# A selective scan laid out by (state, channel) pairs: spread and summed by zero-one matrices on TensorE, product with C on GpSimd, halves of 512 tokens

## The chip, the core and the metric

The kernel runs on one core of a Trainium2 chip. A core has five engines with a queue each, and each queue is worked off in order: TensorE (PE; matrix products, its weight loads are shown apart as PEld), VectorE (DVE), ScalarE (ACT), GpSimd (POOL) and SyncE (SP, here only DMA issues). Engines wait for each other through semaphores. Tensors lie in SBUF, or in PSUM, where matmuls write: eight banks of 512 fp32 columns for each of 128 partitions. GpSimd reads and writes SBUF only.

The metric is the device time of one execution in microseconds (us), median of several runs. A profile of one execution gives the span from the first to the last instruction.

## The reference

Two layers on x of 4 x 256 tokens with 512 features. The first is attention and a gated FFN, the same in both kernels. The second, where the change lies, is a selective state recurrence beside a mixture of LoRA experts:

```python
proj = hidden_states @ in_proj_w            # 512 -> 2*1024
x, z = jnp.split(proj, 2, axis=-1)
xc = silu(conv_b + sum_k conv_w[k] * shifted(x, k))      # 4 taps along time
ssm_p = einsum('bdl,ed->ble', xc, x_proj_w)              # 32 + 16 + 16
dt_r, Bm, Cm = rmsnorm of the three parts
dt = softplus(einsum('blr,dr->bdl', dt_r, dt_proj_w) + dt_bias)
A = -jnp.exp(A_log)                                      # (1024, 16)
def step(h, inp):                                        # along time
    x_t, dt_t, B_t, C_t = inp
    dA = jnp.exp(dt_t[..., None] * A)
    h = dA * h + dt_t[..., None] * B_t[:, None, :] * x_t[..., None]
    y = jnp.einsum('bdn,bn->bd', h, C_t)
    return (h, y)
y = (ys + D_param * xc) * silu(z);  out = y @ out_proj_w
```

There are 1024 channels, 16 states for each, 4 sequences of 256 tokens: 1024 x 16 x 1024 values of h, one after the other along time within each sequence.

## The kernel before

Tiles are declared and the instructions written in program order; a scheduler orders each engine's queue by priorities and its own estimates, so the order in the queues differs from the text. A tile pool has a number of buffers per tag; a new tile waits until its buffer's last reader is done.

Up to L373 layer 0 runs (attention L196 to L280, FFN L282 to L321). At L348 to L371 the weights of layer 1 are loaded and `aneg` (minus exp of A_log) is made, then `down(1)` ends the FFN.

Layer 1 works by sequence (`b`, 256 tokens), channels on partitions in eight chunks (`c`) of 128, taken in pairs:

- `normed` (L391): layer norm and transposes to `xn`.
- `conv_pair` (L396): for two chunks, in-projection on TensorE (L404), a copy and the last tap on ScalarE, three taps on VectorE (L412), silu.
- `ssm_params` (L418): dt_r, B and C; the B and C rows go to DRAM and come back by DMA, copied to all 128 partitions as `rows` (L435 to L442; 8 loads of 512 KB a sequence).
- `gates` (L447): silu(z) for two chunks. `steps` (L458): softplus as a chain over ScalarE and GpSimd (L481 to L486), giving `dt` and `du` = dt * xc.
- `scan_chunk` (L491): a channel per partition. For four groups of four states (`NG`), a tile of 4 x 256 columns: `da` = exp(dt * A) on ScalarE (L501, one activation a state, the first column of each state is kept 0 so that the scan starts anew), `bx` = B * du (L504), the scan `h` (L508), `bx` = h * C (L512), all three on VectorE, and the sum over states as four matmuls with the identity into `y` (L514). At the end y times the gate (L516).
- `experts` (L518), `finish` (L584; out-projection, sum and store).

The loop (L602 to L624) sets the work of the next sequence (convolution, parameters, first steps) between the chunks of this one. PSUM: three banks `mm`, three `s`, two `y`. Three decay buffers, three `bx`, two `h`.

Of the kernel before, what the change touches and what calls it, by code (L numbers as in the profile page):

```python
# [17 lines left out]
P = 128  # L18
# [10 lines left out]
NG = 4  # L29
# [11 lines left out]
def block_kernel(  # L41
# [307 lines left out]
    inx = w1.tile([P, DC, HC, P], F32, name="inx")  # L349
# [17 lines left out]
    ow = w1.tile([P, DC, D], F32, name="ow")  # L367
    nc.sync.dma_start(ow, ow_d)
    aneg = w1.tile([P, DC, NST], F32, name="aneg")
    nc.scalar.activation(aneg, vec[:, :, V_AL : V_AL + NST], AF.Exp)  # L370
# [8 lines left out]
    psmm = ctx.enter_context(tc.tile_pool(name="psmm1", bufs=3, space=PSUM))  # L379
    pss = ctx.enter_context(tc.tile_pool(name="pss", bufs=3, space=PSUM))  # L380
    psy = ctx.enter_context(tc.tile_pool(name="psy", bufs=2, space=PSUM))
    scr = ctx.enter_context(tc.tile_pool(name="scr", bufs=2, space=DRAM))
# [3 lines left out]
    for i in range(3):  # L386
        t = act.tile([P, NG, S], F32, name=f"decay{i}")
        nc.gpsimd.memset(t[:, :, 0:1], 0.0)
        decay.append(t)

    def normed(b):  # L391
        xn = act.tile([P, HC, S], F32, tag="xn1T", name="xn1T", bufs=2)
        layernorm_T((2 * b, 2 * b + 1), act, psmm, xn, 1)
        return xn

    def conv_pair(xn, xc, c0):  # L396

        px = psmm.tile([P, 2, S], F32, tag="mm", name="px")
        pad = act.tile([P, 2, KC - 1 + S], F32, tag="pad", name="pad")
        acc = act.tile([P, 2, S], F32, tag="acc", name="acc")  # L400
        nc.gpsimd.memset(pad[:, :, 0 : KC - 1], 0.0)
        for i in range(2):
            for hc in range(HC):
                mm(px[:, i, :], lhsT=inx[:, c0 + i, hc, :], rhs=xn[:, hc, :],  # L404
                   start=(hc == 0), stop=(hc == HC - 1))
        nc.scalar.copy(pad[:, :, KC - 1 :], px)
        for i in range(2):
            v = vec[:, c0 + i, :]
            nc.scalar.activation(acc[:, i, :], px[:, i, :], AF.Identity, bias=v[:, V_CB : V_CB + 1],  # L409
                                 scale=v[:, V_CW + KC - 1 : V_CW + KC])  # L410
            for k in range(KC - 1):
                nc.vector.scalar_tensor_tensor(  # L412
                    acc[:, i, :], pad[:, i, k : k + S], v[:, V_CW + k : V_CW + k + 1],
                    acc[:, i, :], ALU.mult, ALU.add,
                )
        nc.scalar.activation(xc[:, c0 : c0 + 2, :], acc, AF.Silu)

    def ssm_params(xc):  # L418

        pp = pss.tile([P, S], F32, tag="s", name="pp")  # L420
        for c in range(DC):
            mm(pp[:64, :], lhsT=xpw[:, c, :], rhs=xc[:, c, :], start=(c == 0), stop=(c == DC - 1))  # L422
        sp = act.tile([64, S], F32, tag="sp", name="sp")
        nc.vector.tensor_copy(sp, pp[:64, :])
        sq = act.tile([64, S], F32, tag="sq", name="sq")
        nc.scalar.activation(sq, sp, AF.Square)
        pq = pss.tile([P, S], F32, tag="s", name="pq1")
        mm(pq[:64, :], lhsT=cst[:64, C_BLK : C_BLK + 64], rhs=sq, start=True, stop=True)
        rs = act.tile([64, S], F32, tag="sq", name="rs1")
        nc.scalar.activation(rs, pq[:64, :], AF.Sqrt, bias=eps[:64, 1:2])  # L430
        nc.vector.reciprocal(rs, rs)  # L431
        nrm = act.tile([64, S], F32, tag="nrm", name="nrm", bufs=2)
        nc.vector.scalar_tensor_tensor(nrm, sp, lnw[:, 0:1], rs, ALU.mult, ALU.mult)
        bc = scr.tile([2 * NST, S], F32, tag="bc", name="bc")
        nc.sync.dma_start(bc, nrm[RK:, :])  # L435
        rows = []
        for g in range(NST // NG):
            pair = []
            for k in range(2):
                t = act.tile([P, NG, S], F32, tag=f"bc{g}{k}", name=f"bc{g}{k}")  # L440
                r0 = k * NST + g * NG
                nc.sync.dma_start(t, bc[r0 : r0 + NG, :].partition_broadcast(P))  # L442
                pair.append(t)
            rows.append(pair)
        return nrm, rows

    def gates(xn, c0):  # L447

        sz = act.tile([P, 2, S], F32, tag="sz", name="sz", bufs=2)
        pz = psmm.tile([P, 2, S], F32, tag="mm", name="pz1")  # L450
        for i in range(2):
            for hc in range(HC):
                mm(pz[:, i, :], lhsT=inz[:, c0 + i, hc, :], rhs=xn[:, hc, :],  # L453
                   start=(hc == 0), stop=(hc == HC - 1))
        nc.scalar.activation(sz, pz, AF.Silu)
        return sz

    def steps(nrm, xc, c0):  # L458

        pd = pss.tile([P, 2, S], F32, tag="s", name="pdt")  # L460
        u = act.tile([P, 2, S], F32, tag="u", name="u")
        dt = act.tile([P, 2, S], F32, tag="dt", name="dt", bufs=2)
        dg = act.tile([P, 2, P], F32, tag="dg", name="dg", bufs=2)
        for i in range(2):
            c = c0 + i
            db = vec[:, c, V_DB : V_DB + 1]
            mm(pd[:, i, :], lhsT=dtw[:, c * P : (c + 1) * P], rhs=nrm[0:RK, :],
               start=True, stop=True)
            nc.scalar.activation(u[:, i, :], pd[:, i, :], AF.Abs, bias=db)
            nc.scalar.activation(dt[:, i, :], pd[:, i, :], AF.Relu, bias=db)  # L470
            nc.gpsimd.tensor_scalar(  # L471
                dg[:, i, :], ident, vec[:, c, V_D : V_D + 1], 1.0, ALU.mult, ALU.mult
            )

        nc.scalar.preload_act_table_set("natural_log_exp_and_others")
        nc.scalar.activation(u, u, AF.Exp, scale=-1.0)  # L476
        lw = act.tile([P, 2, S], F32, tag="lw", name="lw")
        nc.scalar.activation(lw, u, AF.Ln, bias=1.0)  # L478

        e = act.tile([P, 2, S], F32, tag="e", name="e")  # L480
        nc.gpsimd.tensor_scalar(e, u, 1.0, -1.0, ALU.add, ALU.add)  # L481
        nc.gpsimd.tensor_tensor(e, u, e, ALU.subtract)
        nc.gpsimd.tensor_tensor(e, e, lw, ALU.add)
        nc.gpsimd.tensor_tensor(dt, dt, e, ALU.add)
        du = act.tile([P, 2, S], F32, tag="du", name="du", bufs=2)
        nc.gpsimd.tensor_tensor(du, dt, xc[:, c0 : c0 + 2, :], ALU.mult)  # L486
        return dt, du, dg
# [3 lines left out]
    def scan_chunk(rows, dt, du, dg, xc, sz, c):  # L491

        y = psy.tile([P, S], F32, tag="y", name="y")
        dt, du, dg = dt[:, c % 2, :], du[:, c % 2, :], dg[:, c % 2, :]
        mm(y, lhsT=dg, rhs=xc[:, c, :], start=True, stop=False)  # L495
        for g in range(NST // NG):
            da = decay[turn[0] % len(decay)]
            turn[0] += 1
            for n in range(NG):
                k = g * NG + n  # L500
                nc.scalar.activation(da[:, n, 1:], dt[:, 1:], AF.Exp,  # L501
                                     scale=aneg[:, c, k : k + 1])
            bx = act.tile([P, NG, S], F32, tag="bx", name="bx", bufs=3)
            nc.vector.tensor_tensor(  # L504
                bx, rows[g][0], du.unsqueeze(1).to_broadcast([P, NG, S]), ALU.mult
            )
            h = act.tile([P, NG, S], F32, tag="h", name="h", bufs=2)
            nc.vector.tensor_tensor_scan(  # L508
                h.rearrange("p n t -> p (n t)"), da.rearrange("p n t -> p (n t)"),
                bx.rearrange("p n t -> p (n t)"), 0.0, ALU.mult, ALU.add,  # L510
            )
            nc.vector.tensor_tensor(bx, h, rows[g][1], ALU.mult)  # L512
            for n in range(NG):
                mm(y, lhsT=ident, rhs=bx[:, n, :], start=False,  # L514
                   stop=(g == NST // NG - 1 and n == NG - 1))
        nc.vector.tensor_tensor(xc[:, c, :], y, sz[:, c % 2, :], ALU.mult)  # L516

    def experts(b, xn):  # L518

        ml = act.tile([P, 2, NE + P], F32, tag="ml", name="ml")  # L520
        for i in range(2):
            pr = pss.tile([P, S], F32, tag="s", name="pr")
            for hc in range(HC):
                mm(pr[:, : NE + P], lhsT=xn[:, hc, i * P : (i + 1) * P], rhs=rl[:, hc, :],
                   start=(hc == 0), stop=(hc == HC - 1))
# [42 lines left out]
        pt = pss.tile([P, S], F32, tag="s", name="pt1")  # L568
# [6 lines left out]
        for i in range(2):  # L575
            tb = 2 * b + i
# [21 lines left out]
    for c in range(0, DC, 2):  # L598
        conv_pair(xn, xc, c)
# [126 lines left out]
```

## Time and profile before

| what | value |
|---|---|
| runs before: median (lowest to highest) | 1273.41 us (1273.18 to 1275.9) |
| profiled execution | 1276.63 us |
| its span | 1274.5 us |
| granted TensorE clock in it, mean | 0.878 |
| busy: PE / PEld | 1046.1 us (82%) / 635.8 us (50%) |
| busy: DVE | 906.6 us (71%) |
| busy: ACT | 550.9 us (43%) |
| busy: POOL | 304.1 us (24%) |

The groups of instructions are rows of the form "line engine operation out<-in partitions x columns, count | busy in us, mean ns of one | idle time of the engine ahead of them, and who ended it". Rows of a stretch give, for each engine, busy time and number of instructions, then the granted clock, the busy share of the DMA engines and GB/s. Rows of the timeline give start, duration, engine, line and operation. fp32 matmuls show as two records each, fp32r matmuls as one. A busy TensorE in the profile is not one at its peak, since ends of matmuls are modelled; distances between starts say more.

### The profile page before, as it was taken

The numbers are of one execution on the slowest core, as the hardware profiler recorded it, in microseconds if no ns is written. First come the engines' busy times: TensorE is split into PE (matmuls) and PEld (weight loads), VectorE is DVE, ScalarE is ACT, GpSimd is POOL, SyncE is SP. The second block draws the span as 40 slices with busy tenths as digits, with TensorE's granted clock in tenths as the row PEclk, the third lists the DMA queues.
The fourth block names the chain that finished last, engine by engine and source line by source line (L and its number), as shares of the span: only waits on it lengthen the run. The fifth ranks groups of instructions, "written<-read, shape, count | busy, mean of one in ns | idle before, by whom it ended". The sixth has DMA issues, their size and how long they took to land.

```text
span 1274.5 us, 10530 instructions
## 1 busy us (share of the span) xinstructions
PE 1046.1 (82%) x3890; PEld 635.8 (50%) x3890; DVE 906.6 (71%) x889; ACT 550.9 (43%) x946; POOL 304.1 (24%) x229
## 2 busy tenths in 40 slices
PE   4999999999999998775677886687877687866697
PEld 1345346634534666553445565444665444554454
DVE  4623613253261315599979999989999979999987
ACT  2133042003304304866435577435577435556341
POOL 2012012001101100513406233506232406184000
PEclk8799599978959998975789899689998789998799
DMA  7112012001101250300000300000300000400000
GB/s 246 34 42 67 17 34 75 1 1 42 51 24 42 94 202 1 134 1 0 1 0 18 132 1 1 1 0 19 132 1 0 1 0 18 132 0 1 0 1 16
DMA packets 18253, 50.28 MB, mean 39 GB/s; under 512 B 2285, under 2 KB 2681, under 8 KB 17562
## 3 DMA queue, kind: packets, MB, share of 16 engines
q1 hardware_dynamic: 8266, 28.91, 6.3%
q0 software_dynamic: 9072, 18.35, 5.1%
q10 hardware_dynamic: 864, 2.36, 0.5%
q8 instruction: 30, 0.49, 0.2%
q14 instruction: 21, 0.17, 0.0%
HBM read 38.21 MB, written 2.23 MB: 32 GB/s over the span
## 4 chain that ended last, share of the span: by engine, by line
DVE 39%; PE 8%; issue 7%; ACT 2%; DVEq 0%; ACTq 0%
DVE h L508 19%; DVE bx L504 10%; DVE bx L512 5%; PE y L514 3%; DVE acc L412 3%; PE po L580 2%; PE pp L422 1%; PE po L578 1%; ACT decay L501 1%; PE po L589 1%; DVE xc L516 1%; ACT L478 1%; DVE rs L431 0%; ACT L501 0%; PE y L495 0%
## 5 line engine op out<-in xcount | busy, mean ns | idle before, releaser
L514 PE MATMUL y<-bx,cst 128*128 128x256 f32 x1024 | 306.1, 454 | 166.5 <-DVE bx L512 166.5
L514 PEld LDWEIGHTS y<-bx,cst 128*128 128x128 f32 x1024 | 220.6, 224 | 255.3 <-DVE bx L512 215.7
L501 ACT ACTIVATE decay<-dt,aneg 128x255 f32<-128x255 f32 x512 | 219.3, 497 | 241.4 <-DVE h L508 212.3
L508 DVE TENSOR_TENSOR_SCAN h<-decay,bx 128x1024 f32<-128x1024 f32 x128 | 310.5, 2431 | 2.2 <-ACT decay L501 1.3
L504 DVE TENSOR_TENSOR bx<-bc,du 128x1024 f32<-128x1024 f32 x128 | 170.4, 1336 | 10.3 <-PE y L514 10.3
L512 DVE TENSOR_TENSOR bx<-h,bc 128x1024 f32<-128x1024 f32 x128 | 170.1, 1334 | 0.1
L305 DVE TENSOR_TENSOR g<-g,pu 128x512 f32<-128x512 f32 x28 | 19.2, 686 | 170.8 <-PE pu L297 170.8
L288 POOL DMA_DIRECT2D wgu<-in_wgu x56 | 29.9, 535 | 379.5 <-PE pg L297 195.5
L471 POOL TENSOR_SCALAR dg<-cst,vec 128x128 f32<-128x128 f32 x32 | 64.2, 2015 | 197.7 <-PE y L495 197.5
L212 PE MATMUL sc<-kbd,q 32*128 32x512 f32 x256 | 101.2, 1009 | 4.4 <-DVE mpl L215 4.4
L303 ACT ACTIVATE g<-pg 128x512 f32<-128x512 f32 x28 | 16.7, 598 | 187.7 <-PE pg L297 187.6
L215 DVE TENSOR_REDUCE mpl<-sc 128x4 f32<-128x1024 f32 x64 | 77.9, 1224 | 28.0 <-PE sc L212 27.8
L481 POOL TENSOR_SCALAR e<-u 128x512 f32<-128x512 f32 x16 | 47.8, 2986 | 193.4 <-ACT u L476 193.4
L265 ACT ACTIVATE pe<-scT 128x1024 f32<-128x1024 f32 x64 | 65.1, 1023 | 59.9 <-PE scT L261 59.9
L261 PE MATMUL scT<-qbd,kT 32*128 32x512 f32 x256 | 71.1, 636 | 0.5
L412 DVE SCALAR_TENSOR_TENSOR acc<-pad,vec,acc 128x256 f32<-128x256 f32 x96 | 56.4, 646 | 19.5 <-ACT acc L409 12.6
L247 PE MATMUL av<-pe,zk 128*32 128x256 f32 x512 | 68.1, 385 | 1.4 <-ACT pe L265 1.4
L212 PEld LDWEIGHTS sc<-kbd,q 32*128 32x128 f32 x256 | 29.9, 279 | 70.9 <-DVE mpl L215 66.8
L453 PE MATMUL pz<-xn1T,inz 128*128 128x256 f32 x256 | 65.1, 401 | 0.0
L589 PE MATMUL po<-ow,xc 128*128 128x512 f32 x128 | 63.3, 617 | 2.2 <-DVE xc L516 2.2
L404 PE MATMUL px<-xn1T,inx 128*128 128x256 f32 x256 | 60.5, 392 | 0.7 <-ACT xn1T L107 0.7
L501 ACT ACT_TABLE_LOAD x44 | 56.5, 1283 | 2.0 <-DVE h L508 1.4
(140 smaller groups left out, 1360.1 us busy)
## 6 DMA issues: line engine op xcount, KB each, us to landing
bc<-bc SPq DMA_DIRECT2D x32, 512.0 KB, 4.6
wgu<-in_wgu POOLq DMA_DIRECT2D x56, 256.0 KB, 2.6
wd<-in_wd POOLq DMA_DIRECT2D x7, 512.0 KB, 6.0
inx<-in_inx SPq DMA_DIRECT2D x1, 2048.0 KB, 9.3
inz<-in_inz SPq DMA_DIRECT2D x1, 2048.0 KB
ow<-in_ow SPq DMA_DIRECT2D x1, 2048.0 KB, 14.7
out<-x SPq DMA_DIRECT2D x8, 256.0 KB, 2.4
x<-in_x ACTq DMA_DIRECT2D x4, 256.0 KB, 3.8
```

The source lines that it names most:

```text
L212: mm(sc[:, j, :], lhsT=q8[r0 : r0 + 32, hf, q0 : q0 + P], rhs=kbd[r0 : r0 + 32, 2 * hp : 2 * hp + 2, :], start=True, stop=True)
L215: nc.vector.tensor_reduce(mpl[:, qb, hf, 2 * gp : 2 * gp + 2, 2 * hp : 2 * hp + 2, 4], sc.rearrange("p j (h k) -> p j h k", h=2), AX.X, AL ...
L247: mm(av[r0 : r0 + 32, hf, :], lhsT=zk[:, 2 * b + c, 24 - 8 * h4 : 56 - 8 * h4], rhs=pe[:, j, i * S : (i + 1) * S], start=(c == 0 and h4 == ...
L261: mm(sc[:, j, :], lhsT=kT[r0 : r0 + 32, k0 : k0 + P], rhs=qbd[hf][r0 : r0 + 32, 2 * hp : 2 * hp + 2, :], start=True, stop=True)
L265: nc.scalar.activation(pe, sc, AF.Exp)
L412: nc.vector.scalar_tensor_tensor(acc[:, i, :], pad[:, i, k : k + S], v[:, V_CW + k : V_CW + k + 1], acc[:, i, :], ALU.mult, ALU.add,)
L501: nc.scalar.activation(da[:, n, 1:], dt[:, 1:], AF.Exp, scale=aneg[:, c, k : k + 1])
L504: nc.vector.tensor_tensor(bx, rows[g][0], du.unsqueeze(1).to_broadcast([P, NG, S]), ALU.mult)
L508: nc.vector.tensor_tensor_scan(h.rearrange("p n t -> p (n t)"), da.rearrange("p n t -> p (n t)"), bx.rearrange("p n t -> p (n t)"), 0.0, A ...
L512: nc.vector.tensor_tensor(bx, h, rows[g][1], ALU.mult)
L514: mm(y, lhsT=ident, rhs=bx[:, n, :], start=False, stop=(g == NST // NG - 1 and n == NG - 1))
L589: mm(po, lhsT=yg[:, c, i * P : (i + 1) * P], rhs=ow[:, c, :], start=(c == 0), stop=(c == DC - 1))
```

## The change

Partitions now hold (state, channel) pairs: 16 states x 8 channels. Tokens go in two halves of 512 (two sequences side by side, `L`), so a chunk of 128 channels is 16 tiles of 512 columns, worked as eight groups (`q`, `half`) of two tiles. dt and du, which lie with a channel per partition, are spread to the pairs by matmuls with a zero-one matrix; each is first split into two fp32r parts, high and low, so that their sum is exact enough. B and C need only one tile per half, made by a matmul with another zero-one matrix (`over`), and the DMA through DRAM goes. The sum over states is a matmul with a third matrix (`gather`) into 32 partitions of y. The product with C moves to GpSimd; B * du is worked in place in PSUM. The zero-one matrices and `aneg` in the new layout are built on the chip ahead of `down(1)`. `wide` gives a bank from the du pool before the first scan ("early") and from a pool of one bank afterwards ("late"). One of the step chain's operations moves from GpSimd to VectorE, as does the diagonal matrix of D. All gates of the next half are made after their chunk's scan. `ow` shares the buffer of `inx` and is loaded late.

```diff
-    ow = w1.tile([P, DC, D], F32, name="ow")
-    nc.sync.dma_start(ow, ow_d)
-    aneg = w1.tile([P, DC, NST], F32, name="aneg")
-    nc.scalar.activation(aneg, vec[:, :, V_AL : V_AL + NST], AF.Exp)
+    spread = w1.tile([P, 4, NST, GC], F32R, name="spread")
+    for r in range(4):
+        rows = slice(32 * r, 32 * r + 32)
+        nc.vector.tensor_copy(spread[rows], ident[rows, rows]
+            .rearrange("p (q e) -> p q e", e=GC).unsqueeze(2).to_broadcast([32, 4, NST, GC]))
+    gather = w1.tile([P, 4, 32], F32, name="gather")
...
+            for i in range(4):
+                nc.tensor.transpose(pa[:, i, :], vec[:, 4 * k + i, V_AL : V_AL + NST], ident)
...
+        for e in range(GC):
+            mm(pa, lhsT=place[:, e].rearrange("p n e -> p (n e)"), rhs=at[:, :, :, e],
+               start=(e == 0), stop=(e == GC - 1))
+        nc.scalar.activation(aneg, pa, AF.Exp)
...
-    psmm = ctx.enter_context(tc.tile_pool(name="psmm1", bufs=3, space=PSUM))
-    pss = ctx.enter_context(tc.tile_pool(name="pss", bufs=3, space=PSUM))
-    psy = ctx.enter_context(tc.tile_pool(name="psy", bufs=2, space=PSUM))
+    psm = ctx.enter_context(tc.tile_pool(name="psm1", bufs=1, space=PSUM))
+    psd = ctx.enter_context(tc.tile_pool(name="psd", bufs=2, space=PSUM))
+    psu = ctx.enter_context(tc.tile_pool(name="psu", bufs=2, space=PSUM))
+    psy = ctx.enter_context(tc.tile_pool(name="psy", bufs=1, space=PSUM))
...
+    def wide(early):
+        if early:
+            return psu.tile([P, 2, L], F32, tag="du", name="early")[:, 0, :]
+        return psm.tile([P, L], F32, tag="mm", name="late")
...
-        bc = scr.tile([2 * NST, S], F32, tag="bc", name="bc")
-        nc.sync.dma_start(bc, nrm[RK:, :])
...
-                nc.sync.dma_start(t, bc[r0 : r0 + NG, :].partition_broadcast(P))
+            mm(pb, lhsT=over[:, k].rearrange("p n e -> p (n e)"), rhs=nrm, start=True, stop=True)
+            t = act.tile([P, L], F32, tag=f"bc{k}", name=f"bc{k}", bufs=2)
+            nc.scalar.copy(t, pb)
...
-        nc.gpsimd.tensor_scalar(e, u, 1.0, -1.0, ALU.add, ALU.add)
+        nc.vector.tensor_scalar(e, u, 1.0, -1.0, ALU.add, ALU.add)
         nc.gpsimd.tensor_tensor(e, u, e, ALU.subtract)
         nc.gpsimd.tensor_tensor(e, e, lw, ALU.add)
         nc.gpsimd.tensor_tensor(dt, dt, e, ALU.add)
+        nc.gpsimd.tensor_tensor(e, dt, xc[:, c, :], ALU.mult)
+        for name, v in (("dt", dt), ("du", e)):
...
+            nc.scalar.copy(hi, v)
+            nc.gpsimd.tensor_tensor(lo, v, hi.bitcast(F32), ALU.subtract)
...
+    def scan_chunk(bc, dt, du, xc, sz, c):
+        y = psy.tile([P, L], F32, tag="y", name="y")
+        skip = act.tile([P, P], F32, tag="skip", name="skip", bufs=2)
+        nc.vector.tensor_scalar_mul(skip, ident, vec[:, c, V_D : V_D + 1])
+        mm(y, lhsT=skip, rhs=xc[:, c, :], start=True, stop=False)
+        for q in range(4):
+            for half in range(2):
+                blocks = [2 * half + i for i in range(2)]
+                def spreads(out, v):
+                    for j in range(2):
+                        for i, r in enumerate(blocks):
+                            rows = slice(32 * r, 32 * r + 32)
+                            mm(out[i], lhsT=spread[rows, q].rearrange("p n e -> p (n e)"),
+                               rhs=v[j][rows, :], start=(j == 0), stop=(j == 1))
+                pds = [psd.tile([P, L], F32, tag="dt", name="pdt") for _ in range(2)]
+                spreads(pds, dt)
+                da = decay[turn[0] % len(decay)]
...
+                    nc.scalar.activation(da[:, i, :, 1:], pds[i]...[:, :, 1:],
+                        AF.Exp, scale=aneg[:, c, 4 * r + q : 4 * r + q + 1])
+                bx = psu.tile([P, 2, L], F32, tag="du", name="bx")
+                spreads([bx[:, 0, :], bx[:, 1, :]], du)
+                nc.vector.tensor_tensor(bx, bx, bc[0]..., ALU.mult)
+                h = act.tile([P, 2, L], F32, tag="h", name="h", bufs=2)
+                nc.vector.tensor_tensor_scan(h..., da..., bx..., 0.0, ALU.mult, ALU.add)
+                hc = act.tile([P, 2, L], F32, tag="hc", name="hc", bufs=2)
+                nc.gpsimd.tensor_tensor(hc, h, bc[1]..., ALU.mult)
+                for i, r in enumerate(blocks):
+                    mm(y[32 * r : 32 * r + 32, :], lhsT=gather[:, q, :], rhs=hc[:, i, :],
+                       start=False, stop=(q == 3))
+        nc.vector.tensor_tensor(xc[:, c, :], y, sz, ALU.mult)
...
     xn, xc = normed(0), new_xc()
+    for c in range(DC):
+        conv(xn, xc, c, True)
+    nrm, bc = ssm_params(xc, True)
+    ready = steps(nrm, xc, 0, True)
+    sz = [gates(xn, c, True) for c in range(DC)]
+    for h in range(2):
+        more = h == 0
+        for c in range(DC):
+            now = ready
+            if c + 1 < DC:
+                ready = steps(nrm, xc, c + 1, False)
+            if c < 2:
+                experts(h, c, xn)
...
+            if more and 2 <= c < 6:
+                conv(xn_next, xc_next, 2 * c - 4, False)
+                conv(xn_next, xc_next, 2 * c - 3, False)
...
+            scan_chunk(bc, *now, xc, sz[c], c)
+            if more and c >= 2:
+                sz[c] = gates(xn_next, c, False)
...
+        finish(h, xc)
```

In the changed file the lines that the prediction names are L460 (the convolution's taps), L470 (gate matmuls), L547 (spreads), L570 (product with C), L574 (gathers), L576 (gate product) and L650 (out-projection).

## Prediction

> **What bounds the kernel now.** I read first the busy time by stretch of the span, then the groups of instructions, then the timeline of one quiet piece.
>
> ```profile
> core 0: us, PE busy (x) PEld busy (x) DVE busy (x) ACT busy (x) POOL busy (x), PEclk, DMA share, GB/s
> 475.00:532.00 57.00, 48.99 (x206) 37.47 (x207) 30.14 (x66) 32.22 (x54) 10.63 (x20) 0.91 0.21 75
> 532.00:680.00 148.00, 98.41 (x305) 65.93 (x304) 137.27 (x121) 82.19 (x157) 41.02 (x22) 0.77 0.00 1
> 870.00:1060.00 190.00, 145.50 (x512) 100.27 (x511) 180.63 (x158) 111.08 (x206) 62.69 (x32) 0.90 0.08 26
> ```
>
> Up to 475 us attention and the FFN run, which the change leaves alone. From the first scan group (532) to the last product with the gate (1267) VectorE is busy 93 to 95%. So 735 of 1274.5 us are paced by one engine.
>
> ```profile
> L508 DVE TENSOR_TENSOR_SCAN h<-decay,bx 128x1024 f32<-128x1024 f32 x128 | 310.5, 2431 | 2.2 <-ACT decay L501 1.3
> L504 DVE TENSOR_TENSOR bx<-bc,du 128x1024 f32<-128x1024 f32 x128 | 170.4, 1336 | 10.3 <-PE y L514 10.3
> L512 DVE TENSOR_TENSOR bx<-h,bc 128x1024 f32<-128x1024 f32 x128 | 170.1, 1334 | 0.1
> ```
>
> These three make 651 us of it, in 128 groups of 1024 columns. The means are inflated; a quiet piece shows the bare price:
>
> ```profile
> 1239.05 2.28 DVE L508 TENSOR_TENSOR_SCAN h<-decay,bx 128x1024 f32<-128x1024 f32 x1
> 1241.25 1.20 DVE L504 TENSOR_TENSOR bx<-bc,du 128x1024 f32<-128x1024 f32 x1
> 1242.36 1.22 DVE L512 TENSOR_TENSOR bx<-h,bc 128x1024 f32<-128x1024 f32 x1
> 1243.50 2.28 DVE L508 TENSOR_TENSOR_SCAN h<-decay,bx 128x1024 f32<-128x1024 f32 x1
> ```
>
> A group takes 4.45 us from scan to scan, of which the product with C (L512) is 1.14. What inflates the means is GpSimd:
>
> ```profile
> 526.23 1.27 POOL L482 TENSOR_TENSOR e<-u,e 128x512 f32<-128x512 f32 x1
> 573.17 3.35 DVE L508 TENSOR_TENSOR_SCAN h<-decay,bx 128x1024 f32<-128x1024 f32 x1
> 574.45 3.13 POOL L483 TENSOR_TENSOR e<-e,lw 128x512 f32<-128x512 f32 x1
> 576.44 1.42 DVE L412 SCALAR_TENSOR_TENSOR acc<-pad,vec,acc 128x256 f32<-128x256 f32 x1
> ```
>
> Alone, a GpSimd product of 512 columns takes 1.27 us. Beside VectorE it takes up to 3.13, and the scan grows by 1.07 (2.28 to 3.35), L412 by 0.95 (0.47 to 1.42): the two take turns.
>
> **The change, part by part.** There are again 128 groups of 1024 columns, so the number of scans stays. Call the steps of a group: spreads D (of dt) and B (of dt·x), exp E, product X with B, scan S, product H with C, gather G.
>
> *VectorE, removed:* H leaves. X and S stay: 4.45 - 1.13 = 3.32 us a group, 425 in all. X now has both its output and one input in PSUM and S one input. No row shows VectorE writing PSUM; L516, which reads y there, costs 0.41 for 256 columns, as much as SBUF copies of that size, so I take no surcharge.
>
> *GpSimd, added:* H of 1024 columns; doubling 1.27 less the 0.10 of a tiny memset gives 2.44 us. Per chunk of eight groups also six products of 512 for the steps (1.27 each), so 27.2 us a chunk against VectorE's 26.6. GpSimd turns from a bystander (24%) into a second pacing engine. Do H and X/S lengthen each other? In the rows only some instructions grew: those with two SBUF inputs, and L97 (one SBUF tensor, 0.54 to 1.42). L90 with one SBUF input stayed at its length beside GpSimd at 475.6, and L516 (PSUM and SBUF, like X and S) took 0.41 beside it at 1120.6. Bounds: 0 to 2 x 1.07 us a group, that is 0 to 274. L516 is nearest in its operands: I take 0. The Trainium skill, "GPSIMD Engine Reference", section 1, puts the contention on VectorE instructions in a two-port mode or with two SBUF inputs, so by it too the term is 0; beside that, section 4.1 advises against two-input products on GpSimd, which it puts at some 2x slower, and by it the 128 products would cost about 128 x 2.4 us there, nearly hidden or not as the loop decides.
>
> *TensorE, added:* eight fp32r matmuls of 32 rows and 512 columns a group and two fp32 gathers into 32 columns. Full fp32r matmuls (L297) follow each other at 0.227 us: 1.82 a group. Attention shows the narrow forms:
>
> ```profile
> 79.07 1.06 PE L247 MATMUL av<-pe,zk 128*32 128x256 f32 x8
> 80.06 1.13 PE L261 MATMUL scT<-qbd,kT 32*128 32x512 f32 x4
> 81.12 1.06 PE L247 MATMUL av<-pe,zk 128*32 128x256 f32 x8
> 82.11 1.13 PE L261 MATMUL scT<-qbd,kT 32*128 32x512 f32 x4
> ```
>
> Each fp32 matmul is two records. Two matmuls of 32 rows take 1.06 here where two full ones (L589, 0.43 a record) take 1.72: neighbours in other row groups overlap. The gather pair has the columns of the eight records of L247: 1.05. Together 2.87 a group; bounds 2.2 (spreads overlapping in pairs as well, 1.15) and 5.1 (a spread at L261's 0.5). The Trainium skill, "TensorEngine Tiling (Array Packing)", section Tiling Modes, says that a change of tiling mode drains the array, against a loop that changes it twice a group; but the period above (2.05) is only 0.1 over eight records at 0.124 and four at 0.24, so the rule is worth 0.05 a change, 13 us in all, not in my sum.
>
> Other TensorE work inside the scan: at 0.86 us for 512 columns in fp32, half 0 holds convolution and gates of half 1 (64, 55 us), experts 22, parameters 10, steps, skip and transposes 15: 102. Half 1 holds experts 22, finish of half 0 (32, 28 us), steps and skip 14: 64. TensorE: 128 x 2.87 + 166 = 534 us. VectorE, GpSimd and TensorE thus all carry 430 to 540 us, where before one carried 700.
>
> *The loop.* The built order puts G of group g behind D and B of g+2, so neighbouring groups do overlap; but decay, h, hc, and both PSUM pools have two buffers, y and the "late" bank have one. Costs that this gives:
> (a) Bare groups: 425. Gate product, skip and the moved e on VectorE: 1.4 a chunk, 22.
> (b) At a chunk's end the gate product L576 stands in VectorE's queue ahead of the next scan in ten of sixteen chunks, and waits for H (2.44) and G (1.05) of the last group, less the X that runs meanwhile (1.13) and some overlap: 2.7 x 10 = 27. Before, two y banks hid this.
> (c) The steps' first three products (3.8 us) stand in GpSimd's queue ahead of an H. S two groups later waits for that H; its slack is 1.13 + 2.2 + 1.13 - 2.55 = 1.9. So 1.9, and 1.1 for the other three: 3.0 x 16 = 48.
> (d) Experts: some 14 small VectorE instructions with two SBUF inputs, each right behind an S, where an H has just begun. L539 grew from 0.16 to 1.23 in that place. At 0.75 of 1.07 each, four times 12: 48.
> (e) Half 1's convolution: 24 L460 at 0.89 + 1.07 (L412 twice, plus the turn) = 47, norm and parameters 12. Its TensorE work (67 with gates) has 47 of slack in six chunks, so 20 show: 79.
> (f) finish of half 0: 28 us of TensorE in one burst with a spread behind it: 28.
> Sum 425 + 22 + 27 + 48 + 48 + 79 + 28 = 677, against 735.
>
> *Before the first group.* TensorE now transposes vec ahead of the last FFN product. Vec landed at 449.7, that product began at 442.35: 7.3 of waiting, and 5 for transposes, copies and eight small matmuls: +12. Convolution for 512 tokens before any scan: L404's 64 records took 16.2 for four pairs, now twice that, +14; parameters at double width (reciprocal 1.75 to 3.4) +3; the 32 gate matmuls stand before the first spread, 28 us, of which steps hide 8: +21. Sum +50: first group at 582. The 33 loads of B and C rows go, but they were hidden behind scans except the first (4.7 us, beside the steps): 0.
>
> *After the last.* finish has one bank: three blocks of 8 x 0.86 with an addition between, 23, beside the 7.2 of before less what its two banks hid: 29 in all.
>
> Sum: 582 + 677 + 29 = 1288 us span, against 1274.5. The profiled execution took 1276.6, 2 more than its span and 3 more than the median, so the span stands one above the median: **1288 us**.
>
> **Rivals.**
> 1. *TensorE paces and the waits hide* (not slower). If (c) to (f) fall into one another's shadow, 534 us of TensorE plus 27 of (b) and half of (c), 24, remain: 585, total 1196. For it: four engines at 60 to 80% with work in other queues. Against: two buffers everywhere, in-order queues. It decides when the scan phase stays under 660, 5.2 us a group.
> 2. *Turns with GpSimd after all*: one lengthening of 1.07 a group is 137, total 1425; two, 1562. L97 speaks for it, L516 against.
> 3. *Spreads at fp32 price*: TensorE 128 x 5.1 + 166 = 819, with (b) 846, total 1457. L297's 0.227 speaks against.
>
> A fully serial loop (1.82 + 1.1 + 3.3 + 2.4 + 1.05, near 10 us) is excluded by the built order.
>
> **How the numbers follow.** A measurement of this kernel tells apart about 0.2%, 2.5 us. Forecast 0.46 (own range 1276 to 1400), rival 1 0.37, the band between 0.03, rival 2 0.08, rival 3 0.06. So faster 0.37, same 0.03, slower 0.60. The range leaves out the end of rival 1 (0.08) and most of rivals 2 and 3 (0.12): 1185 to 1410.
>
> **What would show it.** X near 1.2 and S at 2.28 with H running: no turns; S at 3.3: rival 2. H at 2.4. First X near 582, last gate product 29 before the end. Eight spreads in 1.8. L576 waiting some 2.7 us for TensorE; small expert instructions at 1 us and more. The forecast falls if scans follow at under 5 us through half 0, or if H takes over 3.

## The result, and the profile after

| | before | after |
|---|---|---|
| median (lowest to highest) | 1273.81 us (1273.18 to 1275.9) | 1426.79 us (1419.29 to 1427.92) |
| profiled execution, its span | 1276.63, 1274.5 us | 1419.29, 1417.3 us |
| granted TensorE clock, mean | 0.878 | 0.766 |
| first product with B to last gate product | 532 to 1267: 735 us | 588.3 to 1385.0: 797 us |
| busy: PE, DVE, POOL | 82, 71, 24% | 88, 53, 34% |

The change makes the kernel slower by 11.9%: ratio 1.1185, 95% interval 1.1144 to 1.1226. The forecast (1288 us) had the direction, not the size, and 1427 lies outside its range. The part before the first scan group is 6 us longer than forecast (588 for 582), the part after the last gate product 3 us (32 for 29). The scan phase is 797 us for 677: 120 of the 129 us that the span is off lie there.

These are the groups of instructions of the changed kernel that make the scan (count, then busy us and mean ns of one, then idle time of the engine just before them and who ended most of it):

```profile
L570 POOL TENSOR_TENSOR hc<-h,bc 128x1024 f32<-128x1024 f32 x128 | 303.9, 2379 | 337.9 <-DVE h L565 271.3
L565 DVE TENSOR_TENSOR_SCAN h<-decay,bx 128x1024 f32<-128x1024 f32 x128 | 291.0, 2279 | 14.1 <-ACT decay L555 4.8
L574 PE MATMUL y<-hc,gather 128*32 128x512 f32 x512 | 212.1, 896 | 86.7 <-POOL hc L570 84.8
L561 DVE TENSOR_TENSOR bx<-bx,bc 128x1024 f32<-128x1024 f32 x128 | 156.2, 1225 | 160.8 <-PE bx L547 121.1
L547 PE MATMUL pdt<-dthi,spread 32*128 32x512 f32 x256 | 127.6, 694 | 13.9 <-ACT decay L555 10.9
```

Scan and product with B last 2279 and 1225 ns, their bare price before, so VectorE is not slowed down. It is idle: 160.8 us ahead of the product with B, mostly until TensorE has written `bx`. TensorE in turn stood idle 84.8 us ahead of a gather until GpSimd was done.

The busy time by stretch shows the second thing that was not forecast. Columns as before; the first row is the first quarter of the scan phase, the second its end, where almost no other work is left:

```profile
588.00:780.00 192.00, 160.10 (x466) 61.81 (x462) 130.61 (x122) 77.11 (x115) 95.91 (x54) 0.70 0.00 1
1240.00:1385.00 145.00, 125.69 (x381) 36.97 (x381) 108.99 (x66) 40.95 (x66) 83.79 (x40) 0.60 0.00 0
```

TensorE is busy for 83 and 87% of the time, at a granted clock of 0.70 and 0.60.

And the timeline of a gap between scans (start, duration, engine, line; idle time before and who ended it in brackets):

```profile
1102.57 2.29 DVE L565 TENSOR_TENSOR_SCAN h<-decay,bx 128x1024 f32<-128x1024 f32 x1
1105.44 3.60 PE L641 MATMUL late<-bw,xn1T 128*128 128x512 f32 x8
1108.97 1.06 PE L574 MATMUL y<-hc,gather 128*32 128x512 f32 x6
1110.92 3.60 PE L641 MATMUL late<-bw,xn1T 128*128 128x512 f32 x8
1115.43 0.49 PE L547 MATMUL pdt<-dtlo,spread 32*128 32x512 f32 x1
1116.02 0.69 ACT L555 ACTIVATE decay<-pdt,aneg 128x510 f32<-128x510 f32 x1 [11.37 <-PE pdt L547]
1118.00 2.29 DVE L565 TENSOR_TENSOR_SCAN h<-decay,bx 128x1024 f32<-128x1024 f32 x1
```

The low part of `dt` for one block (1115.43) stands in TensorE's queue behind two blocks of the experts' base products (L641) and the gathers between them. ScalarE waits 11.4 us for it, and from one scan to the next 15.4 us go by, where 3.5 would do. TensorE is at full clock through both blocks (3.60 us for eight records); only the first 2.6 of the 15.4 us ran at half clock. So most of this gap has nothing to do with the clock.

### The profile page after: what moved, and what is told of

The parts are those of the page before. It is cut to its first block, busy times and chain, and to the rows that moved or that the text cites. A ratio compares the mean times of both kernels' runs of the same rounds, so it can differ in the third digit from the quotient of the medians.

```text
span 1417.3 us, 10856 instructions
## 1 busy us (share of the span) xinstructions
PE 1240.9 (88%) x4082; PEld 510.5 (36%) x4082; DVE 756.9 (53%) x738; ACT 472.4 (33%) x646; POOL 479.8 (34%) x341
## 4 chain that ended last, share of the span: by engine, by line
PE 67%; DVE 12%; POOL 12%; issue 4%; ACT 3%; DMA 1%; POOLq 0%; DVEq 0%; SPq 0%; ACTq 0%
PE y L574 10%; POOL hc L570 8%; PE sc L213 7%; DVE h L565 6%; PE late L650 5%; PE scT L262 5%; PE av L248 5%; PE pdt L547 4%; PE bx L547 4%; PE pg L298 4%; PE po L320 4%; PE pu L298 3%; PE late L470 2%; PE early L470 2%; PE early L449 2%
## 5 line engine op out<-in xcount | busy, mean ns | idle before, releaser
L570 POOL TENSOR_TENSOR hc<-h,bc 128x1024 f32<-128x1024 f32 x128 | 303.9, 2379 | 337.9 <-DVE h L565 271.3
L565 DVE TENSOR_TENSOR_SCAN h<-decay,bx 128x1024 f32<-128x1024 f32 x128 | 291.0, 2279 | 14.1 <-ACT decay L555 4.8
L574 PE MATMUL y<-hc,gather 128*32 128x512 f32 x512 | 212.1, 896 | 86.7 <-POOL hc L570 84.8
L555 ACT ACTIVATE decay<-pdt,aneg 128x510 f32<-128x510 f32 x256 | 164.7, 683 | 358.8 <-PE pdt L547 309.4
L561 DVE TENSOR_TENSOR bx<-bx,bc 128x1024 f32<-128x1024 f32 x128 | 156.2, 1225 | 160.8 <-PE bx L547 121.1
L547 PE MATMUL pdt<-dthi,spread 32*128 32x512 f32 x256 | 127.6, 694 | 13.9 <-ACT decay L555 10.9
L547 PE MATMUL bx<-duhi,spread 32*128 32x512 f32 x256 | 105.2, 591 | 10.5 <-DVE h L565 10.1
L547 PE MATMUL bx<-dulo,spread 32*128 32x512 f32 x256 | 106.2, 585 | 0.0
L547 PE MATMUL pdt<-dtlo,spread 32*128 32x512 f32 x256 | 102.9, 582 | 0.0
L216 DVE TENSOR_REDUCE mpl<-sc 128x4 f32<-128x1024 f32 x64 | 77.9, 1225 | 28.0 <-PE sc L213 27.9
L574 PEld LDWEIGHTS y<-hc,gather 128*32 128x32 f32 x512 | 23.1, 129 | 175.3 <-POOL hc L570 135.9
L547 PEld LDWEIGHTS pdt<-dthi,spread 32*128 32x128 f32 x256 | 47.1, 253 | 104.0 <-issue 56.8
L547 PEld LDWEIGHTS bx<-duhi,spread 32*128 32x128 f32 x256 | 47.5, 258 | 64.9 <-issue 41.9
L650 PE MATMUL late<-ow,xc 128*128 128x512 f32 x128 | 67.5, 675 | 3.2 <-DVE x L652 2.3
L547 PEld LDWEIGHTS bx<-dulo,spread 32*128 32x128 f32 x256 | 49.0, 262 | 54.0 <-issue 49.4
```

The source lines that it names most:

```text
L216: nc.vector.tensor_reduce(mpl[:, qb, hf, 2 * gp : 2 * gp + 2, 2 * hp : 2 * hp + 2, 4], sc.rearrange("p j (h k) -> p j h k", h=2), AX.X, AL ...
L547: mm(out[i], lhsT=spread[rows, q].rearrange("p n e -> p (n e)"), rhs=v[j][rows, :], start=(j == 0), stop=(j == 1))
L555: nc.scalar.activation(da[:, i, :, 1:], pds[i].rearrange("p (b t) -> p b t", b=2)[:, :, 1:], AF.Exp, scale=aneg[:, c, 4 * r + q : 4 * r + ...
L561: nc.vector.tensor_tensor(bx, bx, bc[0].unsqueeze(1).to_broadcast([P, 2, L]), ALU.mult)
L565: nc.vector.tensor_tensor_scan(h.rearrange("p i t -> p (i t)"), da.rearrange("p i b t -> p (i b t)"), bx.rearrange("p i t -> p (i t)"), 0. ...
L570: nc.gpsimd.tensor_tensor(hc, h, bc[1].unsqueeze(1).to_broadcast([P, 2, L]), ALU.mult)
```

## The experiments

Three theories were set up first. FORMS: TensorE's clock stays low since 32-row spreads and 32-column gathers do not count as enough work, and a group so costs it twice the price. GAPS: the clock is low because TensorE waits between groups. LOOP: the clock matters little, the scans wait for what stands in TensorE's queue. LOOP was later split in two: TRIP (the gather waits for the product with C on GpSimd, and the next spreads stand behind it) and BURST (runs of other matmuls stand ahead of the spreads).

Where no range or interval stands, the time is that of one execution; the kernel before took 1274 to 1279 us beside them. The changed kernel's 1427 is what they are compared with.

### The clock by itself: streams of matmuls

```diff
+    for k in range(160): mm(p[k % 2], lhsT=full, rhs=vr)
+    for k in range(160): mm(p[k % 2], lhsT=spread[32 rows of block k % 2], rhs=vr[same rows])
+    for k in range(80): mm(p[2][32 rows of block k % 2], lhsT=ident[:, 32 columns], rhs=vf)
+    for k in range(12): eight spreads, two gathers
...
```

> Leaves out the whole computation (the output is the input x): only streams of matmuls run, each after a pause of some 10 us. In order: 160 full fp32r products of 128 rows; 160 fp32r spreads of 32 rows in two row groups by turns; 80 fp32 gathers into 32 columns; 12 times eight spreads and two gathers; 80 fp32 spreads of 32 rows; 12 times four fp32 spreads and two gathers; a loop of eight spreads and two gathers that wait for two ScalarE copies; the same loop with full products. Theory FORMS (the clock stays low because 32-row fp32r products and 32-column gathers do not count as enough work): full products granted 0.9 or more after their first microseconds, spreads and the mixed stream 0.6 or less though nothing waits; the narrow loop 0.6 or less, the full loop 0.85 or more. Theory GAPS (the clock falls where TensorE waits between groups): every stream without waits is granted 0.85 or more, narrow or full, and both loops 0.5 to 0.75 alike. Theory LOOP (the clock has little to do with it) says nothing of the clock, but then eight spreads and two gathers without waits should take well under 6 us at whatever clock.

The timeline of its TensorE (rows of one stream run together; all operations of a kind have one line, L113 full, L120 spreads, L127 gathers):

```profile
28.73 39.04 PE L113 MATMUL p<-vr,full 128*128 128x512 f32 x160 [13.60 <-ACT vr L109]
178.59 2.08 PE L120 MATMUL p<-vr,spread 32*128 32x512 f32 x8
180.60 1.92 PE L127 MATMUL p<-vf,cst 128*32 128x512 f32 x2
424.05 1.19 PE L120 MATMUL p<-vr,spread 32*128 32x512 f32 x8
425.51 1.53 PE L127 MATMUL p<-hc,cst 128*32 128x512 f32 x4 [0.28 <-ACT hc L169]
```

and its granted clock by stretch: spreads alone, gathers alone, the mixed stream, the end of the narrow loop:

```profile
90.00:115.00 25.00, 24.80 (x118) 18.72 (x114) 0.00 (x0) 0.17 (x1) 0.00 (x0) 0.50 0.00 0
127.00:165.00 38.00, 37.48 (x160) 9.46 (x160) 0.00 (x0) 1.43 (x3) 0.00 (x0) 0.92 0.00 1
176.70:225.00 48.30, 48.15 (x144) 16.27 (x144) 0.00 (x0) 2.99 (x4) 0.00 (x0) 0.50 0.00 0
414.00:436.00 22.00, 19.69 (x85) 6.55 (x83) 0.00 (x0) 9.45 (x18) 0.00 (x0) 1.00 0.00 0
```

Spreads, and spreads mixed with gathers, stay at 0.50 for 25 and 48 us in which TensorE is never idle; fp32 products of 32 rows did the same for 69 us. Full products started 0.427 us apart for the first 5.3 us of their stream and 0.227 us apart after that; gathers rose to 1.00 after 6 us. So GAPS falls: no gap, half the clock; and the narrow loop, which does wait (0.28 us a round), ended at 1.00. FORMS holds for 32 rows and falls for gathers, which by themselves had 0.92 over the stretch. The narrow loop went up after 19 us; why it did where the mixed stream did not stays open.

The prices: full fp32r products 0.227 us each at full clock, 1.82 for eight (39.04 / 160 = 0.244 has the slow start in it). Eight 32-row spreads 2.07 us at half clock, 1.19 at full clock, since neighbours overlap in pairs; two gathers 1.92 and, at full clock, 1.05 (a row of o6 below).

### Wider matrices in the changed kernel

```diff
-    mm(out[i], lhsT=spread[rows, q]..., rhs=v[j][rows, :], ...)
+    mm(out[i], lhsT=spread[:, 4 * r + q]..., rhs=v[j], ...)          # e1, e2: zero rows elsewhere
-    mm(y[32 * r : 32 * r + 32, :], lhsT=gather[:, q, :], rhs=hc[:, i, :], ...)
+    mm(y, lhsT=gather[:, q] with zero columns elsewhere, rhs=hc[:, i, :], ...)   # e2 only
```

> The spreads use all 128 rows (the zero-one matrix padded with zero rows; same count, same result), nothing else of weight changes. FORMS: the granted clock between first and last scan goes from 0.66 to 0.85 or more, eight spreads take 1.8 to 2.1 us instead of 3.45, the time falls to 1290 us (1250 to 1340). GAPS: the clock stays under 0.75; eight spreads that no longer overlap in pairs take 8 x 0.4 = 3.2 us or more, the time stays 1420 or grows to 1480. LOOP: the time moves by less than 20 us.

> Spreads over all 128 rows and gathers over all 128 columns (zero-padded; some scratch buffers of the convolution shared to make room). FORMS: clock 0.9 or more in the scan, 1.82 + 1.72 = 3.54 us a group on TensorE, 128 of them and 166 of other work make 619 us, under the scan phase that the other engines need (about 680): 1290 us (1260 to 1340). GAPS: clock 0.6 to 0.75, so 3.54 / 0.68 = 5.2 us a group, 666 + 244 = 910 us of TensorE: 1500 us or more. LOOP: 1420 to 1450.

> dt and du are spread whole in fp32 with 32 rows (two passes each), without the split into parts: half the spread instructions, 32 ScalarE copies and 32 GpSimd subtractions (1.27 us each) fewer. Attention's rows show this form beside 32-column products at granted clock 1.00 with TensorE fully busy. FORMS in the version that fp32r with 32 rows is what does not count: clock 0.85 or more, 2.12 + 1.05 = 3.2 us a group, time 1270 to 1310. FORMS for all narrow products: clock 0.6 to 0.7, 3.2 / 0.65 = 4.9 us a group, time 1380 to 1440. GAPS: clock 0.6 to 0.75 as well, time 1380 to 1440. LOOP: GpSimd gives 2.54 us a chunk back, the time falls by 20 to 40 to 1385 to 1405.

| run | time | granted clock |
|---|---|---|
| changed kernel | 1426.79 | 0.766 |
| e1: spreads over 128 rows | 1394.01 | 0.905 |
| e2: and gathers over 128 columns | 1514.40 | 0.916 |
| e3: fp32 spreads of 32 rows, no split | 1652.42 | 0.728 |

Full rows do lift the clock (0.91 to 0.98 in the stretches of the scan phase), as FORMS said, and the time falls by 33 us, not by 130: none of the three theories has the number. With the clock up, the gaps are still there: from the scan at 1091.8 to the next 15.3 us go by, with the same two blocks of L637 (the changed kernel's L641) ahead of the same spread. e2 is worse by 120 us at the same clock. Its gathers are dearer, and its built queue is another one, so it does not tell the two apart: in the changed kernel 83 of the 128 gathers have at least a part of a second group's spreads of `du` ahead of them (33 have all of it), in e2 40 (15). e3 loses 226 us. Its spreads are dearer (four fp32 ones took 3.78 us in the streams at half clock, against 2.07 for the change's eight), but in its built queue only 2 gathers have any of a second group ahead, so it does not separate price from order either.

Between, as a finer test of the clock, two of the eight spreads were made full and six left narrow:

```diff
+    if j == 0 and v is dt:
+        rows = slice(0, P)
```

> As the changed kernel, but two of a group's eight spreads (the high part of dt) use all 128 rows; the other six keep 32. In the streams measured alone, gathers at half of TensorE's time left the clock at 0.50 and at 53% raised it; here full-row work is 63% of a group. FORMS: the clock in the scan rises to 0.85 or more, and eight spreads then cost 6 x 0.15 + 2 x 0.23 = 1.35 us, 0.5 less than eight with full rows: 1340 to 1385, below the 1394 of full rows. If the clock stays low: 1405 to 1430.

1462.79 us at a clock of 0.788 (0.65 to 0.76 in the stretches of the scan phase): neither. So the share of full-row work does not decide the clock alone, and in a built queue that is nearly the same in all three (83 or 84 gathers as above), the mixed form takes longer than either.

### Taking away what the gathers wait for, or a burst

```diff
-    nc.gpsimd.tensor_tensor(hc, h, bc[1]..., ALU.mult)      # d1, d2: left out, gathers read h
+    nc.vector.tensor_tensor(hc, h, bc[1]..., ALU.mult)      # d3
-    if c < 2: experts(h, c, xn)                             # d4
```

> The product with C is left out; the gathers sum h itself. Everything else is the changed kernel (spreads over 32 rows). Theory TRIP (what the clock does not explain is the way through GpSimd: the gather waits for the product with C in TensorE's in-order queue, and the next spreads stand behind it): the gather can start 2.4 us earlier in every group; if TensorE's clock stayed low it would carry 2.07 + 1.92 = 4.0 us a group, 510 us, and twice 166 of other work, so no more than 40 us come off: 1380 to 1420. If the clock rises because fewer waits remain: 1290. Theory BURST (other matmuls in TensorE's queue, in runs of 4 to 9 us, delay the scans, since only two groups can be ahead): under 30 us come off: 1390 to 1420.

> Spreads over all 128 rows, and the product with C left out. The kernel with full-row spreads took 1394 us, and GpSimd's product holds 140 us of its chain that ended last. TRIP: 100 us or more come off, to 1250 to 1300. BURST: the long gaps between scans (8 to 17 us, twice or so a chunk) stay, and 20 to 60 come off: 1335 to 1375.

> Spreads over all 128 rows, the product with C on VectorE (1.13 us) instead of GpSimd (2.39). VectorE then carries 4.45 us a group, 570 us, and some 45 of other work. TRIP: the way from scan to gather is 1.25 us shorter a group and GpSimd no longer stretches VectorE's small instructions: 30 to 80 us come off, 1315 to 1365. BURST: VectorE's 145 us more lie partly in the gaps: 1390 to 1430.

> Spreads over all 128 rows; the experts of the second layer are left out (their matmuls, 45 us of TensorE in all, and their small VectorE instructions). BURST: the first two chunks of each half lose their gaps of 10 to 17 us: 60 to 90 us come off, 1305 to 1335, more than the 45 us that the matmuls take and though TensorE is idle 12% of the scan. TRIP: 45 us at the most come off, 1350 to 1385.

d1: 1347.60, 79 us less than the changed kernel; d2: 1290.16, 104 less than e1; d3: 1353.83, 40 less than e1; d4: 1330.93, 63 less than e1. Without the wait for GpSimd 104 us go, as TRIP said; without the experts 63 go for 45 us of matmuls, as BURST said. d1's 79 us lie between TRIP's two numbers, 40 at a low clock and 137 at a high one; the clock in the scan phase rose from 0.69 to 0.76. d3 puts 145 us more on VectorE and still gains 40, so VectorE had the time. That the way through GpSimd was on the path is not shown by it: the scheduler built other queues in d1 to d3, and in d3 90 gathers have two whole groups' spreads of `du` ahead, in e1 33.

### The same operations in another order

If TRIP and BURST are both features of the order in TensorE's queue, a better order should remove them without changing one operation. In the next kernels every engine's queue in the scan phase is written out by hand:

```diff
+    for s in range(128):
+        read_bank()             # what reads the one "late" bank (second order)
+        spreads of dt for s + 2; exponentials of s + 2
+        product with C of s (GpSimd)
+        spreads of du for s + 2
+        product with B and scan of s + 1
+        at most four matmuls of something else
+        gathers of s
```

> The same operations as the kernel with full-row spreads, but every engine's queue in the scan phase is written out by hand, group by group: spreads of group g+2, at most four other matmuls (experts, convolution, parameters, gates, out-projection in turn), then the gathers of g; VectorE: product with B and scan of g+1; GpSimd: product with C of g and at most one product of the softplus chain. No burst stands ahead of spreads and every gather has two groups of spreads ahead of it. Theory ORDER (what is left beside the clock is how the built order makes TensorE's queue wait): TensorE carries 1.82 + 1.05 + 0.1 = 3.0 us a group and 1.2 us of other work, 4.2 x 128 = 538 us; with 592 before and 32 after: 1160 (1130 to 1220), below the kernel before the change. Theory BUFFERS (two groups ahead are too few in any order, since a gather waits for product, scan and product with C): 1300 or more.

> The same hand-written queues with the change's own spreads of 32 rows. FORMS: spreads and gathers make 2.07 + 1.92 = 4.0 us a group at half clock, and 1.2 us of other work takes 2.4: 6.4 x 128 = 819, 1440 us if the clock stays low all along; with the clock at 0.7 as in the first half now, 1250 to 1320. In any case slower than full rows in the same order by 60 us or more, though at full clock the pairs are cheaper (1.2 against 1.9 us for eight). If the clock is not what matters once the order is right: within 20 us of the full rows, or faster.

> The hand-written queues with full-row spreads, the product with C on VectorE. VectorE carries 4.45 us a group (570 us) and some 60 us of other work, 630 in all: 592 + 630 + 32 = 1254 (1230 to 1290), slower than with GpSimd by 60 to 100 us. If the way through GpSimd were what costs even in this order, it would be faster than with GpSimd.

o1: 1343.46 us (ratio to before 1.0546, 1.0522 to 1.0570); o2, with narrow spreads, 1352.99 (1.0613, 1.0594 to 1.0633); o3 1395.64. o1 is better than e1 by 51 us, but by ORDER's number a miss by 180; it lies where BUFFERS had it. o2 is within 10 us of o1, though its clock in the scan phase was 0.77 and o1's 0.92. o3 has o1's queue on TensorE and loses 52 us with the product with C on VectorE: in this order the way through GpSimd is not what costs. The timeline of o1 shows why (a helper records all operations, so they have one line; tiles tell them apart):

```profile
789.72 0.63 ACT L438 ACTIVATE xc<-acc 128x512 f32<-128x512 f32 x1
793.32 0.78 ACT L438 ACTIVATE acc<-late,vec 128x512 f32<-128x512 f32 x1
794.15 6.77 PE L438 MATMUL late<-xn1T,inx 128*128 128x512 f32 x8 [5.93 <-ACT acc L438]
```

The next convolution's matmuls wait 5.9 us for the one bank, because ScalarE reads it only behind exponentials, a silu and its table loads; behind those matmuls stand the gathers and the next spreads. The second order puts every reader of that bank first:

> The mixed spreads in a second hand-written order: as the first, but whatever reads the one bank of the other matmuls stands ahead of the exponentials in ScalarE's queue and ahead of product and scan in VectorE's, the convolution's taps behind the scan, its matmuls two a group. TensorE 1.35 + 1.05 + 0.15 = 2.55 us a group and 1.3 of other work, 493 us; VectorE 3.5 us a group and 60 of other work, 508. ORDER: 592 + 510 to 600 + 32 = 1135 to 1225. BUFFERS: still over 1300.

> The second hand-written order with full-row spreads. TensorE 3.0 + 1.3 = 4.3 us a group, 550 us: 20 to 60 us above the mixed spreads if TensorE's price a group sets the time (ORDER with FORMS), within 10 of them if it does not.

> The second hand-written order with the change's spreads of 32 rows. FORMS: where no other matmul runs beside the groups the clock is 0.5 and a group costs TensorE 4.0 us and more instead of 2.4: 30 to 80 us above the mixed spreads. If the order alone matters: within 10 us of them.

| second hand-written order | time | ratio to before | granted clock |
|---|---|---|---|
| o4: mixed spreads | 1268.30 | 0.9941 (0.9924 to 0.9957) | 0.878 |
| o5: spreads over 128 rows | 1276.35 | | 0.912 |
| o6: spreads of 32 rows, as in the change | 1252.95 | 0.9823 (0.9808 to 0.9838) | 0.846 |

TensorE's idle time ahead of matmuls into the one bank fell from 76 us (o1) to 25 (o5), and the time by 67; so BUFFERS falls too, though o4's forecast by ORDER (1135 to 1225) is missed. o6 has the change's own matrices and operations (beside eight ScalarE copies more and a few shared scratch buffers) and takes 174 us less than the built order, 1.8% less than the kernel before. FORMS said it would be 30 to 80 us above o4; it is 15 below, and with the lowest clock of the three the fastest.

What sets most of the time is the order, of all engines' queues together. The cleanest pair is e1 and o5: spreads over 128 rows in both, a clock of 0.93 and 0.94 in the scan phase, and 118 us less. From the changed kernel to o6 the clock in the scan phase rose with the order, from 0.69 to 0.81, so a part of the 174 us may be the clock's; no run has 32-row spreads at full clock throughout. Two rows of the waits (us in total, times, the longest), first of the changed kernel, then of o6:

```profile
DVE bx L561 <- PE bx L547: 121.1, 47, 30.8
PE y L574 <- POOL hc L570: 84.8, 60, 4.3
```

```profile
DVE bx L441 <- PE bx L441: 8.3, 12, 1.7
PE y L441 <- POOL hc L441: 28.4, 25, 4.3
```

VectorE hardly waits for `bx` any more. A piece of o6's timeline, with four records of gate matmuls in it:

```profile
934.06 2.29 DVE L441 TENSOR_TENSOR_SCAN h<-decay,bx 128x1024 f32<-128x1024 f32 x1
935.86 1.05 PE L441 MATMUL y<-hc,gather 128*32 128x512 f32 x4
936.26 1.21 DVE L441 TENSOR_TENSOR bx<-bx,bc 128x1024 f32<-128x1024 f32 x1
936.85 0.49 PE L441 MATMUL pdt<-dthi,spread 32*128 32x512 f32 x2
937.60 2.29 DVE L441 TENSOR_TENSOR_SCAN h<-decay,bx 128x1024 f32<-128x1024 f32 x1
```

Scan to scan takes 3.54 us here, the bare price of product with B and scan (the forecast had 3.32). The scan phase is 585.6 to 1215.7, 630 us instead of 797.

Last, each feature of the built order was put back:

```diff
+    o7: four pieces of other matmuls together in every fourth group, none in the others
+    o8: gathers of s ahead of the spreads of s + 2 instead of behind them
```

> The second hand-written order with 32-row spreads (1253 us), but the other matmuls stand in bursts: four pieces together (up to ten matmuls, 4 to 9 us) in every fourth group, none in the others. BURST: two groups of spreads ahead are 7 us of scans, a burst with its waits for the one bank takes longer: 1330 to 1400. TRIP: under 40 us more, 1260 to 1290.

> The second hand-written order with 32-row spreads (1253 us), but a group's gathers stand ahead of the spreads of two groups later instead of behind them, so TensorE's queue has one group of spreads less ahead while it waits for GpSimd. TRIP: from the end of a scan 2.4 for the product with C, 1.05 to 1.9 for the gathers, 1.2 to 2.1 for spreads, then the product with B: 4.7 to 6.4 us before the scan after next has its input, against 3.5, and the other matmuls come on top: 1360 to 1450. BURST: under 40 us more, 1260 to 1290.

o7: 1400.02, 147 us more than o6. o8: 1384.19, 131 more. The same two rows of the waits, of o7 and then of o8:

```profile
DVE bx L441 <- PE bx L441: 66.5, 20, 11.9
PE y L441 <- POOL hc L441: 104.6, 50, 6.7
```

```profile
DVE bx L441 <- PE bx L441: 89.4, 55, 4.9
PE y L441 <- POOL hc L441: 134.0, 61, 5.8
```

Each takes back most of the 174 us, and they cannot simply be added, since 147 and 131 make 278. Two things moved with them. The clock in the scan phase fell back as well (0.71 and 0.73, for 0.81 in o6), and how much of the time that is was not measured. And o7 lets the readers of the one bank stand further back again; TensorE's idle time ahead of that bank grew only from 33 to 45 us.

## Why the prediction was wrong

- *Prices on VectorE and GpSimd, the turns*: right, but for one. Product with B 1225 ns, scan 2279, product with C 2379 for 2.44 us forecast; the longest of 128 scans lasted 2290 ns and the longest product with B 1233, in a phase with 304 us of products with C, so the term for turns is 0, as taken. The rule of the Trainium skill on instructions with two SBUF inputs ("GPSIMD Engine Reference", section 1) agrees: the experts' small ones (L607, L609) grew from 0.16 to a mean of 0.89 and 0.80 us, as in (d). The one is (a): a bare group was taken as 3.32 us, from rows in which another product stands between the product with B and its scan. Where the scan follows its product directly, as 123 times in o6, the starts are 1.35 us apart and not 1.13. A group so takes 3.54, and 128 x 0.22 = 28 us of the 120 can be this.
- *Before the first group, after the last*: 588 for 582, 32 for 29.
- *The chunk's end (b)*: L576 waited 27.9 us for TensorE, 27 forecast. The mechanism was right; that the sums agree is partly luck, since there were 14 waits of 2.0 us on average and not ten of 2.7.
- *TensorE's price, 2.87 us a group*: the mechanism (overlap in pairs) was taken for fp32 and left out for fp32r. Eight spreads cost 1.19 us at full clock, near the lower bound, and 2.07 at half clock. Two gathers cost 1.05 or 1.92. So 2.24 or 4.0, not 2.87. The rows that I priced with came from attention at full clock; that the clock is a part of the price was not in the sum. This step was wrong, but it isn't most of the 120 us: with the clock up 33 go (e1, whose spreads cost 1.82 a group), and at a mean clock of 0.846 o6 runs the same matrices in 1253.
- *The loop, (b) to (f)*: the step that failed. It began "The built order puts G of group g behind D and B of g+2, so neighbouring groups do overlap", and then added waits to VectorE's bare 447 us: 27 + 48 + 48 + 79 + 28 = 230. Measured: 797 - 447 = 350, the 28 us of the dearer bare group among them. The sentence is true as it stands for 33 of 128 gathers; 50 have only a part of B of g+2 ahead, 39 at most B of g+1, and 6 not even a part of that. o8 shows that one group less costs 131 us where it is so everywhere. And (e) and (f) counted TensorE's other work by its sum against slack ("20 show") or as one burst at the end of a half; what counts is how long a run ahead of a spread is, since with two buffers the scans live on two groups, 7 us. The experts' two runs of five matmuls (4.6 us each at full clock, gathers between them) were not in the sum as a wait at all; o7 shows that runs of that kind in every fourth group cost 147 us.
- *Rivals*: rival 1 (TensorE paces and the waits hide, 1196) did not happen, but o6's 1253 lies on its way: it names the right condition, the waits. Rival 3 (1457) has nearly the time, by the wrong road: TensorE's price at half clock was 4.0 us a group, not its 5.1, and TensorE was busy for 676 us of the scan phase, not 819; and o5, with the clock up and dearer spreads, and o6 differ by 23 us, the orders by 118 to 174. Rival 2 fell with the turns.

What is not settled: how the 174 us divide between gathers, bursts and the clock within the built order, and by which rule the clock goes up.

## What to carry to other kernels

Where a loop runs over engines in turn with two buffers, read the built order of the pacing queue first: for each instruction that waits for another engine count what stands behind it, and for each run of foreign work how long it is against what the buffers hold. Sums of busy time did not tell the two apart here: the same operations took 630 us of scan phase in one order and 797 in another. And a price read from a trace holds for the clock that it was read at: look for the same form elsewhere in the trace at another clock.

## What the runs showed of the hardware

- A stream of 32-row matmuls (fp32r or fp32) stayed at half clock here, however dense: 0.50 over 25 us of spreads and 69 us of fp32 products. The profile of the kernel before had a hint of it: the scores' matmuls (L212, 32 rows, no gathers among them) have a mean of 1009 ns, attention's L261, of the same shape but mixed with 32-column products, 636. The Trainium skill, "TensorE: Matmul & The Clock Gate", Part 1, says that about 3.4 us of sustained work release the clock; the full stream here, at full clock after 5.3 us, agrees, the 32-row streams do not.
- Two 32-row fp32r matmuls in different row groups overlap as fp32 ones do: eight in 1.19 us at full clock, against 1.82 for eight full ones.
- A group that changes between full-row and 32-row spreads is slower than with either kind in the built order (1463 for 1394 and 1427); in the second hand-written order it lies between (1268 for 1276 and 1253).
- Two VectorE instructions start some 0.2 us further apart when the second reads what the first writes: product with B to its scan 1.35 us (o6), to another product 1.12 (d3); scan to its own product with C 2.39 (o3), to another product 2.20 (kernel before).
